# Arrays laid out in DRAM as on chip, with fewer loads, LoRA A summed on GpSimd and a planner that takes copy destinations in advance

## The chip, the cores and the metric

The kernel runs on one core of a Trainium2 chip. The metric is the device time of one execution in microseconds (us). The engines are called as in the profile: PE is TensorE (PEld its weight loads), DVE is VectorE, ACT is ScalarE, POOL is GpSimd, and SP is SyncE, which issues every load and store of this kernel.

## What is computed

The inputs are x (4 batches of 256 tokens with 512 features), a context of 64 rows per batch, four 256x256 side matrices per batch index (used as block weights) and a mask over the context rows. Four layers follow one another; the last two are the same function with the same arguments.

```python
# layer 0: routed LoRA; lora_A is the context, summed over its 4 batches
w   = softmax(x @ router_W.T + router_b)             # 8 experts
a   = einsum('bsh,arh->bsr', x, ctx)                 # x @ (sum of ctx over a).T
y   = einsum('bsr,nhr->bsnh', a, lora_B)
x   = nan_to_num(x + 0.5 * einsum('bsn,bsnh->bsh', w, y))
# layer 1: cross attention to ctx, 32 heads of 16, masked, then layer norm
x   = layernorm(x + attend(x @ Wq.T + bq, ctx @ Wk.T + bk, ctx @ Wv.T + bv, mask) @ Wo.T + bo) * ln_g + ln_b
# layers 2 and 3: 4 blocks each over the 8 nearest neighbours of the
# context's 512 columns; x is seen as 256 channels by 512 points
idx = top_k(-distance(ctx columns), 8)
for i in range(4):
    p = leaky_relu(x)
    x = (f[i] @ p + (f[i] @ gather(p, idx)).sum(8)) / 9 + x
```

## The kernel before

**Planner.** The kernel does not fix the order of its instructions by hand. Each step is added to a `Plan` with its engine, an estimated cost, what it reads and what it writes (`add`, L63). `emit` (L84) then plays the steps through: every engine has a time at which it is free, a step can start when its inputs are there and when its buffers have places, and among the steps of an engine that could start within 0.05 us of the earliest, the one with the lowest rank is issued. The rank is the due time of the batch, `DEADLINES = (0.0, 20.0, 40.0, 45.0)` (L32), minus the length of the work that still hangs on the step. A load's end is estimated from one pipe (L129). Buffers (`Buf`) come from pools with a fixed number of places: 8 PSUM banks, 5 halves (`half`, 128x512 f32), 4 `pT`, 8 `wp` and so on. A place is taken when the first step that names the buffer is issued. The result is one fixed queue of instructions per engine. On the chip each engine works through its queue in order and waits on semaphores where an operand is not ready.

**Loads.** SP issues all loads in the order in which the code lists them (L237 to L262). Most arrays are kept in the DRAM as plain matrices and are rearranged by the access pattern. xT, ctxT and the side matrices `fT` come in runs of 1 KB, weights and x in runs of 2 KB; the router's weights in runs of 32 bytes and the biases `bqk` in runs of 16 bytes.

**Work of one batch.** `mixture` multiplies xT by the router weights and the summed context (`route`, L327), takes a softmax over 8 experts on DVE and ACT (L341 to L352), forms `z` (L357), transposes it (`zT`, L375, copied by ACT, L380) and multiplies it by lora_BT (`upd`, L385). DVE adds the result to x (L400) and cleans it of NaNs with POOL's help (L406 to L410); a transpose gives `x1T` (L414, L420), and POOL adds bo (L426). `queries` makes the queries (`q`, L580), `values` the values (`v`, L542, put into `vbd` by DVE, L560), `keys` once the keys of all batches (`kT`, L488, spread by POOL into `kbd`, L511). `attention` scores (`s`, L610 and L621), takes the softmax (DVE L647, L653, L662, L668, L674; ACT L659; POOL L683), transposes (`pT`, L695, L700), and applies values (`avT`, L707, L721) and output weights (`o`, L727), followed by the layer norm (L739 to L752). `nearest` copies the context (`cxl`, POOL L431; its square, ACT L430), computes distances (`d`, L439), picks eight neighbours with DVE (`top` L445, `rest` L448, `near` L454) and turns the choice into a matrix `nbr` (L466 to L472). Each of 32 `block` steps computes the leaky ReLU on DVE (`p`, L765), a product with the side matrix (`wp`, L776), splits it into a high part (ACT, L789) and a low part (DVE, `wpl`, L792), gathers through `nbr` (`blk`, L807) and adds (DVE, L819).

The context summed over the batches (LoRA A) is one DVE reduction at L301, and the router's weights land straight beside it in the tile `rw`, so that one matmul gives logits and LoRA product:

```python
V_.tensor_reduce(rw[:, :, NB:], ctxT.rearrange("p c b v -> p c v b"), AX.X, ALU.add)
```

Of the kernel before, what the change touches and what calls it, by code (L numbers as in the profile page):

```python
# [18 lines left out]
V, R = 64, 64  # L19
# [12 lines left out]
DEADLINES = (0.0, 20.0, 40.0, 45.0)  # L32
# [5 lines left out]

class Buf:


    def __init__(self, kind, name):
        self.kind, self.name, self.users, self.left, self.tile = kind, name, [], 0, None
# [6 lines left out]
class Plan:  # L50
# [7 lines left out]
    def __init__(self, places, make):  # L58
        self.places = {k: [(0.0, i) for i in range(n)] for k, n in places.items()}
        self.make, self.ops, self.wrote, self.read = make, [], {}, {}  # L60
        self.batch, self.unit, self.pipe = 0, None, 0.0
# [22 lines left out]
    def emit(self, deadline):  # L84
# [16 lines left out]
        while ready:  # L101
            best = {}
            for op in ready:
                t = max([free[op.eng]] + [o.end + (SEEN[o.eng] if o.eng != op.eng else 0.0) for o in op.before])
                want = {}
                for k in op.bufs:
                    if k.tile is None:
                        want[k.kind] = want.get(k.kind, 0) + 1
# [6 lines left out]
            for eng, found in best.items():  # L115
                first = min(t for t, _ in found)
                t, op = min((f for f in found if f[0] <= first + 0.05), key=lambda f: (f[1].rank, f[1].n))
# [3 lines left out]
            for k in op.bufs:  # L121
                if k.tile is None:
                    self.places[k.kind].sort()
                    _, k.place = self.places[k.kind].pop(0)
                    k.tile = self.make(k.kind, k.place, k.name)
            op.fn()
            free[op.eng] = op.end = t + op.cost
            if op.load:
                self.pipe = op.end = max(op.end + 1.6, self.pipe) + op.load / 0.33  # L129
            for k in op.bufs:  # L130
                k.left -= 1
                if not k.left:
                    self.places[k.kind].append((op.end + (0.0 if op.load else SEEN[op.eng]), k.place))
# [8 lines left out]
def xattn_seq_kernel(ctx: ExitStack, tc: tile.TileContext, a: dict, out: bass.AP):  # L142
# [27 lines left out]
    plan = Plan({kind: n for kind, (_, _, _, n) in shapes.items()}, make)  # L170
# [29 lines left out]
    rbb = const.tile([128, NB], F32, name="rbb")  # L200
    bqk = const.tile([128, 2, NC], F32, name="bqk")
    mask_i = const.tile([128, B, V], I32, name="mask_i")
    rows = {n: const.tile([128, H], F32, name=n) for n in ("bv", "bo", "ln_g", "ln_b")}
# [19 lines left out]
    xT_src = a["xT"].rearrange("(c p) t -> p c t", p=128)  # L223
    x_src = a["x"].rearrange("(b l p) h -> b p l h", p=128, l=NL)

    def load_xT(b):

        after = (("x1T", 1, 0),) if b == B - 1 else ()
        load(xT[b], 0.5, lambda: xT[b].tile, xT_src[:, :, b * S : (b + 1) * S], after)

    def load_x(b):
        load(("x", b), 0.5, lambda: x1[b], x_src[b])

    def load_w(n):
        load(n, 1.0, lambda: w[n], a[n].rearrange("(c p) o -> p c o", p=128))

    load(("cxx", 0), 0.13, lambda: cxx[0][0:64], a["ctx"][0])  # L237
    load("ctxT", 0.5, lambda: ctxT, a["ctxT"].rearrange("(c p) (b v) -> p c b v", p=128, v=V))
    load("rw", 0.02, lambda: rw[:, :, 0:NB], a["router_WT"].rearrange("(c p) n -> p c n", p=128))
    load_xT(0)  # L240
    load("rbb", 0.01, lambda: rbb, a["router_b"].partition_broadcast(128))
    load_w("lora_BT")
    load_x(0)
    load("bqk", 0.02, lambda: bqk, a["bqk"].rearrange("k p c -> p k c"))
    for b in range(1, B):
        load(("cxx", b), 0.13, lambda b=b: cxx[b][0:64], a["ctx"][b])
    load("mask_i", 0.12, lambda: mask_i.rearrange("p b v -> p (b v)"), a["mask"].partition_broadcast(128))
    for c in range(NC):
        load(("WkT", c), 0.25, lambda c=c: WkT[c], a["WkT"][bass.ts(c, 128), :])
    load_w("WqT")  # L250
    load_w("WvT")
    load("bv", 0.25, lambda: rows["bv"], a["bv"].partition_broadcast(128))
    load_xT(1)
    load_x(1)
    load("bo", 0.25, lambda: rows["bo"], a["bo"].partition_broadcast(128))
    load_w("WoT")
    load("ln_g", 0.25, lambda: rows["ln_g"], a["ln_g"].partition_broadcast(128))
    load("ln_b", 0.25, lambda: rows["ln_b"], a["ln_b"].partition_broadcast(128))
# [630 lines left out]
```

## Time and profile before

| | us |
|---|---|
| median of 3 runs | 423.57 (423.35 to 423.77) |
| profiled execution, device time | 422.2 |
| its span, first to last instruction | 420.5 |
| PE busy | 400.4 (95%) |
| DVE busy | 287.6 (68%) |
| ACT busy | 115.0 (27%) |
| POOL busy | 93.8 (22%) |

The mean granted TensorE clock of the profiled execution is 0.992. The DMA queues move 15.19 MB in it, nearly all of the loads in the first 45 us. Busy time of an engine is the time that its instructions cover; matmuls are pipelined, and their ends are modelled. In the timeline each row has its start and its length in us, engine, line, operation, tiles and number of instructions; brackets hold the idle time of the engine just before, and what ended it. A float32 matmul appears as two instructions. In the chain of waits each row has a start, a length, and the engine and line that the end of the kernel hung on at that time.

### The profile page before, as it was taken

The page shows a single profiled execution, that of the slowest core. Times are in us where ns is not written, and L with a number is a line of the kernel's source. Part 1 is how long each engine was busy: PE and PEld are TensorE (multiplying, and loading weights), DVE is VectorE, ACT ScalarE, POOL GpSimd, SP SyncE. Part 2 cuts the span into 40 slices and gives each one's busy share as a digit, 9 for nine tenths or more (in the row PEclk, how much of TensorE's full clock was granted, in tenths as well). Part 3 has the DMA queues.
Part 4 walks back from the last instruction along what each step waited for, and adds up shares of the span by engine and source line. Part 5 has one row for each costly group of instructions (what it writes and reads, how often), then busy time and mean ns, then how long its engine had stood idle before and what let it go on. Part 6 is the DMA issues. An engine that isn't in the chain of part 4 may idle for free.

```text
span 420.5 us, 5667 instructions
## 1 busy us (share of the span) xinstructions
PE 400.4 (95%) x2288; PEld 305.8 (73%) x2288; DVE 287.6 (68%) x495; ACT 115.0 (27%) x210; POOL 93.8 (22%) x94
## 2 busy tenths in 40 slices
PE   5499998999999999988999999999999999999996
PEld 3358864678666588757758678788888888888885
DVE  4581699956999876999796676855546565555552
ACT  1203432611365023523445121131111112121211
POOL 4129031660306550263435022000000000000000
PEclk9799999999999999999999999999999999999999
DMA  6999200000000000000000000000100000000002
GB/s 201 251 343 354 67 0 2 2 1 0 2 1 2 2 0 2 0 2 0 2 2 2 0 0 0 2 0 2 50 1 2 0 2 0 25 27 0 0 2 100
DMA packets 10617, 15.19 MB, mean 36 GB/s; under 512 B 1504, under 2 KB 5216, under 8 KB 10592
## 3 DMA queue, kind: packets, MB, share of 16 engines
q1 hardware_dynamic: 10592, 14.84, 10.8%
q8 instruction: 18, 0.29, 0.3%
q14 instruction: 7, 0.06, 0.0%
HBM read 12.74 MB, written 2.10 MB: 35 GB/s over the span
## 4 chain that ended last, share of the span: by engine, by line
PE 81%; DVE 10%; DMA 2%; ACT 2%; SPq 2%; issue 1%; POOL 1%; ACTq 0%; DVEq 0%
PE blk L807 27%; PE wp L776 24%; PE o L727 7%; PE upd L385 6%; PE q L580 5%; PE pT L695 2%; DMA cxx<-in_ctx 2%; DVE p L765 2%; SPq L219 2%; PE d L439 2%; PE avT L707 1%; DVE den L662 1%; PE s L621 1%; DVE mx L647 1%; PE x1T L414 1%
## 5 line engine op out<-in xcount | busy, mean ns | idle before, releaser
L776 PE MATMUL wp<-fT,p 128*128 128x256 f32 x512 | 116.8, 380 | 1.5 <-DVE wpl L792 1.5
L807 PE MATMUL blk<-nbr,wph 128*128 128x512 f32 x256 | 107.8, 421 | 1.5 <-DVE wpl L792 1.5
L776 PEld LDWEIGHTS wp<-fT,p 128*128 128x128 f32 x512 | 96.2, 190 | 17.1 <-DVE wpl L792 1.9
L807 PE MATMUL blk<-nbr,wpl 128*128 128x512 f32 x256 | 100.5, 393 | 0.1
L789 ACT CAST wph<-wp 128x512 fp32r<-128x512 f32 x64 | 37.4, 585 | 161.5 <-PE wp L776 156.2
L792 DVE TENSOR_TENSOR wpl<-wp,wph 128x512 fp32r<-128x512 f32 x64 | 44.0, 690 | 49.7 <-ACT wph L789 49.4
L819 DVE SCALAR_TENSOR_TENSOR x<-blk,x 128x512 f32<-128x512 f32 x64 | 43.9, 687 | 36.3 <-PE blk L807 36.2
L807 PEld LDWEIGHTS blk<-nbr,wph 128*128 128x128 f32 x256 | 48.1, 188 | 13.8 <-DVE wpl L792 1.9
L807 PEld LDWEIGHTS blk<-nbr,wpl 128*128 128x128 f32 x256 | 48.2, 188 | 11.3 <-DVE wpl L792 0.6
L765 DVE SCALAR_TENSOR_TENSOR p<-x 128x512 f32<-128x512 f32 x64 | 50.4, 796 | 7.2 <-POOL x L752 5.8
L683 POOL TENSOR_TENSOR s<-s,rden 128x512 f32<-128x512 f32 x32 | 36.3, 1165 | 83.9 <-DVE rden L674 72.0
L385 PE MATMUL upd<-lora_BT,zTs 128*128 128x512 f32 x64 | 29.6, 606 | 0.9 <-ACT avTs L721 0.8
L647 DVE TENSOR_REDUCE mx<-s 128x8 f32<-128x512 f32 x32 | 19.8, 682 | 14.3 <-PE s L621 14.3
L727 PE MATMUL o<-WoT,avTs 128*128 128x512 f32 x64 | 29.0, 594 | 0.0
L580 PE MATMUL q<-x1T,WqT 128*128 128x256 f32 x128 | 28.5, 380 | 0.4 <-ACT x1T L420 0.4
L580 PEld LDWEIGHTS q<-x1T,WqT 128*128 128x128 f32 x128 | 24.2, 190 | 4.3 <-ACT x1T L420 0.6
L439 PE MATMUL d<-cxx,cxl 128*128 128x512 f32 x32 | 18.2, 698 | 7.3 <-POOL cxl L431 7.3
L700 ACT COPY pTs<-pT 128x512 f32<-128x512 f32 x32 | 17.1, 595 | 24.7 <-PE pT L695 24.1
L385 PEld LDWEIGHTS upd<-lora_BT,zTs 128*128 128x128 f32 x64 | 12.2, 197 | 13.7 <-issue 12.3
L727 PEld LDWEIGHTS o<-WoT,avTs 128*128 128x128 f32 x64 | 11.8, 190 | 12.3 <-issue 11.9
L662 DVE TENSOR_REDUCE den<-s 128x8 f32<-128x512 f32 x32 | 19.8, 678 | 0.3 <-ACT s L659 0.3
L653 DVE TENSOR_TENSOR s<-s,mx 128x512 f32<-128x512 f32 x32 | 20.0, 682 | 0.0
(86 smaller groups left out, 372.2 us busy)
## 6 DMA issues: line engine op xcount, KB each, us to landing
xT<-in_xT SPq DMA_DIRECT2D x4, 512.0 KB, 8.1
x<-in_x SPq DMA_DIRECT2D x4, 512.0 KB, 10.3
out<-x SPq DMA_DIRECT2D x8, 256.0 KB, 2.0
lora_BT<-in_lora_BT SPq DMA_DIRECT2D x1, 1024.0 KB, 11.0
WkT<-in_WkT SPq DMA_DIRECT2D x4, 256.0 KB, 4.9
WqT<-in_WqT SPq DMA_DIRECT2D x1, 1024.0 KB, 7.5
WvT<-in_WvT SPq DMA_DIRECT2D x1, 1024.0 KB, 9.5
WoT<-in_WoT SPq DMA_DIRECT2D x1, 1024.0 KB, 12.4
```

The source lines that it names most:

```text
L385: T_.matmul(ps2.tile, lhsT=zT.tile[:, bass.ts(c, 128)], rhs=w["lora_BT"][:, c, :], start=(c == 0), stop=(c == NC - 1),)
L439: lambda ps=ps, j=j: T_.matmul(ps.tile, lhsT=cxl[b][:, bass.ts(j, 128)], rhs=cxx[b], start=True, stop=True),
L580: T_.matmul(ps.tile[:, 0:S], lhsT=w["WqT"][:, c, bass.ts(o, 128)], rhs=x1T[b].tile[:, c, :], start=(c == 0), stop=(c == NC - 1),)
L647: lambda mx=mx, ps=ps: V_.tensor_reduce(mx.tile[:, 0:HPC], heads(ps), AX.X, ALU.max),
L683: lambda s=s, g=g: G_.tensor_tensor(heads(s), heads(s), rden.tile[:, bass.ts(g, HPC)].unsqueeze(2).to_broadcast([128, HPC, V]), ALU.mult,),
L727: T_.matmul(po.tile, lhsT=avT.tile[:, bass.ts(c, 128)], rhs=w["WoT"][:, c, :], start=(c == 0), stop=(c == NC - 1),)
L765: lambda l=l: V_.scalar_tensor_tensor(p.tile[:, l], pt[:, l], SLOPE, pt[:, l], ALU.mult, ALU.max),
L776: T_.matmul(ps.tile[:, bass.ts(k, S)], lhsT=p.tile[:, c, bass.ts(2 * m2 + k, 128)], rhs=wi[:, c, :], start=(c == 0), stop=(c == NL - 1),)
L789: act(0.59, lambda ps=ps, hi=hi: A_.copy(hi.tile, ps.tile), (ps,), (hi,))
L792: lambda ps=ps, hi=hi, lo=lo: V_.tensor_tensor(lo.tile, ps.tile, hi.tile.bitcast(F32), ALU.subtract),
L807: T_.matmul(pb[o].tile, lhsT=part.tile[:, bass.ds(m % 2 * S + o * 128, 128)], rhs=nbr[b, m], start=(m == 0 and k == 0), stop=(m == H // 12 ...
L819: lambda o=o: V_.scalar_tensor_tensor(pt[:, o], pb[o].tile, 1.0 / (KNN + 1.0), pt[:, o], ALU.mult, ALU.add),
```

## The change

The host lays the arrays out so that each partition's share is one run: 4 KB for xT, ctxT and x, 8 KB for lora_BT, the weights and the side matrices, with WkT still taken in four loads of 2 KB runs. Router weights, router_b and the q and k biases become one array `small` (192 bytes per partition), bv and bo one (`rows1`), ln_g and ln_b one (`rows2`). The context of batch 1 is loaded ahead of lora_BT, and the mask behind WqT. Since the router's weights no longer land in `rw`, ACT copies them there. The sum for LoRA A is made by three GpSimd additions of 128x256, with one `half` buffer for the two partial sums. In the planner, loads are modelled with eight in flight at a rate of 0.3 in place of 0.33, due times are changed, the 0.05 us tolerance is dropped, a second kind of place (`stage`, 8 of them) is counted beside the PSUM banks of all steps but the blocks, and several matmul steps name the SBUF buffer into which their PSUM result will be copied, so that its place is taken with the matmul. `values` names `vbd` in its matmul as well.

```diff
-DEADLINES = (0.0, 20.0, 40.0, 45.0)
+DEADLINES = (0.0, 5.0, 45.0, 50.0)
...
+LANES = 8
+RATE = 0.3
...
-                t = max([free[op.eng]] + [o.end + (SEEN[o.eng] if o.eng != op.eng else 0.0) for o in op.before])
+                t = free[op.eng] if not op.load else max(free[op.eng], self.landed[-LANES])
+                t = max([t] + [o.end + (SEEN[o.eng] if o.eng != op.eng else 0.0) for o in op.before])
...
-                t, op = min((f for f in found if f[0] <= first + 0.05), key=lambda f: (f[1].rank, f[1].n))
+                t, op = min((f for f in found if f[0] <= first), key=lambda f: (f[1].rank, f[1].n))
...
-                self.pipe = op.end = max(op.end + 1.6, self.pipe) + op.load / 0.33
+                op.end = max(op.end + 1.4, self.landed[-1]) + op.load / RATE
+                self.landed.append(op.end)
...
-    plan = Plan({kind: n for kind, (_, _, _, n) in shapes.items()}, make)
+    plan = Plan({kind: n for kind, (_, _, _, n) in shapes.items()} | {"stage": 8}, make)
...
-        load(xT[b], 0.5, lambda: xT[b].tile, xT_src[:, :, b * S : (b + 1) * S], after)
+        load(xT[b], 0.5, lambda: xT[b].tile.rearrange("p c t -> p (c t)"), a["xT"][b], after)
...
-        load(n, 1.0, lambda: w[n], a[n].rearrange("(c p) o -> p c o", p=128))
+        load(n, 1.0, lambda: w[n].rearrange("p c o -> p (c o)"), a[n])

     load(("cxx", 0), 0.13, lambda: cxx[0][0:64], a["ctx"][0])
-    load("ctxT", 0.5, lambda: ctxT, a["ctxT"].rearrange("(c p) (b v) -> p c b v", p=128, v=V))
-    load("rw", 0.02, lambda: rw[:, :, 0:NB], a["router_WT"].rearrange("(c p) n -> p c n", p=128))
+    load("ctxT", 0.5, lambda: ctxT.rearrange("p c b v -> p (c b v)"), a["ctxT"])
+    load("small", 0.05, lambda: consts, a["small"])
     load_xT(0)
-    load("rbb", 0.01, lambda: rbb, a["router_b"].partition_broadcast(128))
+    load(("cxx", 1), 0.13, lambda: cxx[1][0:64], a["ctx"][1])
     load_w("lora_BT")
     load_x(0)
-    load("bqk", 0.02, lambda: bqk, a["bqk"].rearrange("k p c -> p k c"))
-    for b in range(1, B):
+    for b in range(2, B):
         load(("cxx", b), 0.13, lambda b=b: cxx[b][0:64], a["ctx"][b])
+    for c in range(NC):
+        load(("WkT", c), 0.25, lambda c=c: WkT[c], a["WkT"][:, bass.ts(c, H)])
+    load_w("WqT")
     load("mask_i", 0.12, lambda: mask_i.rearrange("p b v -> p (b v)"), a["mask"].partition_broadcast(128))
-    for c in range(NC):
-        load(("WkT", c), 0.25, lambda c=c: WkT[c], a["WkT"][bass.ts(c, 128), :])
-    load_w("WqT")
     load_w("WvT")
-    load("bv", 0.25, lambda: rows["bv"], a["bv"].partition_broadcast(128))
+    load("rows1", 0.5, lambda: rows1, a["rows1"].partition_broadcast(128))
     load_xT(1)
     load_x(1)
-    load("bo", 0.25, lambda: rows["bo"], a["bo"].partition_broadcast(128))
     load_w("WoT")
-    load("ln_g", 0.25, lambda: rows["ln_g"], a["ln_g"].partition_broadcast(128))
-    load("ln_b", 0.25, lambda: rows["ln_b"], a["ln_b"].partition_broadcast(128))
-    load("fT", 1.0, lambda: fT, a["fsideT"].rearrange("i (c p) o -> p i c o", p=128))
+    load("rows2", 0.5, lambda: rows2, a["rows2"].partition_broadcast(128))
+    load("fT", 1.0, lambda: fT.rearrange("p i c o -> p (i c o)"), a["fsideT"])
...
     def lora_a():
-        dve(
-            1.9,
-            lambda: V_.tensor_reduce(rw[:, :, NB:], ctxT.rearrange("p c b v -> p c v b"), AX.X, ALU.add),
-            ("ctxT",),
+        act(
+            0.25,
+            lambda: A_.copy(rw[:, :, 0:NB], consts[:, 0 : NC * NB].rearrange("p (c n) -> p c n", n=NB)),
+            ("small",),
+            ("rw",),
+        )
+        part = Buf("half", "lora_a")
+
+        def half(k):
+            return part.tile[:, k * 256 : (k + 1) * 256].rearrange("p (c v) -> p c v", v=V)
+
+        for k in range(2):
+            pool(
+                0.66,
+                lambda k=k: G_.tensor_tensor(half(k), ctxT[:, :, 2 * k, :], ctxT[:, :, 2 * k + 1, :], ALU.add),
+                ("ctxT", part),
+                (("part", k),),
+            )
+        pool(
+            0.66,
+            lambda: G_.tensor_tensor(rw[:, :, NB:], half(0), half(1), ALU.add),
+            (part, ("part", 0), ("part", 1)),
             ("rw_a",),
         )
...
             (("z", b, l), zb, "ident"),
-            (ps,),
+            (ps, zT),
...
             ("WvT", "ctxT"),
-            (ps,),
+            (ps, ("vbd", b % 2)),
```

The copy's buffer is named in the same way in the matmul steps of `pT` (L695), `avT` (L707) and `wp` (L776, with both the high and the low part).

## The prediction

> **What bounds the kernel now.** I read the page first, then a table of engine time by stage, then the waits, the timeline and the chain of waits of the first 60 us. The page's first part names the bound.
>
> ```profile
> span 420.5 us, 5667 instructions
> PE 400.4 (95%) x2288; PEld 305.8 (73%) x2288; DVE 287.6 (68%) x495; ACT 115.0 (27%) x210; POOL 93.8 (22%) x94
> ```
>
> PE is busy for 400.4 of 420.5 us, so 20.1 us of idle PE, and whatever PE does slowly, is all that can be won without removing matmuls; the change removes none. The stage table, cut where the trace changes character, says where those 20.1 us lie (busy us per engine, then granted clock, DMA share, GB/s).
>
> ```profile
> 0.00:20.43 20.43, 10.56 (x34) 6.08 (x35) 9.41 (x23) 4.51 (x7) 6.81 (x22) 0.86 0.79 224
> 20.43:45.65 25.22, 24.59 (x134) 18.24 (x133) 11.08 (x23) 5.43 (x11) 12.97 (x12) 0.98 0.88 304
> 45.65:90.00 44.35, 42.03 (x321) 27.52 (x322) 41.99 (x83) 17.95 (x35) 16.52 (x14) 1.00 0.05 13
> 90.00:250.00 160.00, 156.45 (x1039) 115.45 (x1038) 129.35 (x220) 57.07 (x106) 52.25 (x43) 1.00 0.00 1
> 250.00:416.40 166.40, 166.40 (x766) 138.55 (x764) 94.96 (x148) 30.07 (x53) 5.25 (x4) 1.00 0.03 10
> 416.40:420.50 4.10, 0.36 (x2) 0.00 (x0) 0.84 (x2) 0.00 (x0) 0.00 (x0) 1.00 0.33 128
> ```
>
> Stage length minus PE busy: 9.87, 0.63, 2.32, 3.55, 0 and 3.74 us. Half is in the first 20 us. The timeline and the chain of waits show why.
>
> ```profile
> 4.30 5.48 PE L439 MATMUL d<-cxx,cxl 128*128 128x512 f32 x8 [4.30 <-POOL cxl L431]
> 9.62 1.90 PE L327 MATMUL route<-rw,xT 128*128 128x72 f32 x16
> 14.07 0.66 PE L375 MATMUL zT<-ident,z 128*128 128x128 f32 x4 [2.56 <-DVE z L357]
> 17.74 2.05 PE L439 MATMUL d<-cxx,cxl 128*128 128x512 f32 x2 [3.01 <-POOL cxl L431]
> 20.43 7.62 PE L385 MATMUL upd<-lora_BT,zTs 128*128 128x512 f32 x16
> 4.87 2.77 SPq L219 DMA_DIRECT2D bqk<-in_bqk  x1
> 7.68 9.31 DMA cxx<-in_ctx
> 17.05 0.61 POOL cxl L431
> ```
>
> PE starts at 4.30, as soon as the first context is copied. It idles 2.56 us for z, which comes from a chain of small DVE operations, and then 3.01 us because the next instruction in its queue is a distance matmul of batch 1, whose context was issued behind lora_BT, x and bqk and lands only at 16.99. `upd` stands behind it. lora_BT is no excuse: issued at 3.65 with 11.0 us to landing, it is there at 14.65.
>
> **Change, part by part.** *Order of the loads.* The context of batch 1 moves ahead of lora_BT, into the place where router_b was issued at 3.11. xT of batch 0, just ahead of it, lands at 7.96 (2.56 + 5.4). With 128 KB more I put cxx1 at 8.5 to 9.5; router_b itself, in that place, landed at 10.7 (3.11 + 7.6), which is my late end. POOL's copy (0.60) and ACT's square (0.63) follow, so the distances of batch 1 can start between 9.1 and 11.3, before route ends at 11.52 (9.62 + 1.90). They are 8 matmul instructions of 0.43 us, 3.4 us in all, and fill PE while DVE makes z. z is ready at 14.0 as now: its chain from route is unchanged, and DVE's interleaved match is worth at most 0.7 us either way. Then zT (0.43), ACT's copy (0.59) and handovers: `upd` starts at 15.2 to 15.8, and I take 15.5 instead of 20.43: 4.9 us. With lora_BT at 14.65, or later by the 0.4 us that 128 KB cost at 300 GB/s, this still holds. By then three quarters of the batch-1 distance matmuls, which now run at 53.64 (six instructions, 2.6 us), are also behind us; the 4.9 us count the displacement of `upd`, and this is extra work pulled forward, worth up to 2.6 us if the stage at 45 to 90 us stays full.
>
> *Clock.* The granted clock fell in the gaps:
>
> ```profile
> 12.00:16.00 4.00, 0.66 (x4) 0.42 (x4) 2.52 (x8) 0.22 (x1) 0.00 (x0) 0.85 0.95 192
> 16.00:20.00 4.00, 2.26 (x4) 1.15 (x5) 1.41 (x4) 2.39 (x4) 1.76 (x3) 0.50 0.80 255
> 20.00:24.00 4.00, 4.00 (x11) 2.06 (x10) 3.99 (x12) 0.59 (x1) 0.00 (x0) 0.80 1.01 336
> ```
>
> Sixteen `upd` matmuls took 7.62 us where the steady 0.43 us give 6.9: 0.7 us to win. The two slow distance matmuls (2.05 for 0.86) lie inside the interval already counted. [...] The row shows 0.50 directly behind the two gaps with 0.66 us of work between, so I take the row: front gain 5.6.
>
> *LoRA A on GpSimd.* Removed: one DVE reduction, 1.93 us from 5.74. Added: three POOL adds of 128x256. The nearest row is POOL's 128x512 add at 1327 ns (L408), half of it 0.66 each, 2.0 in sum; the strided 128x256 product at 1005 ns (L511) gives 3.0 as the high end. ctxT lands at 5.7, so the sum is ready at 7.7 to 8.7, later than now or equal, but before route's 9.62, held by PE's own distances. [...] If POOL's three remaining memsets go first (they end at 6.42 now), 8.4 to 9.4, still in time. ACT gains one copy of 128x32, near the 0.22 us of its small exponent, before route, on an engine that is idle from 4.2 to 12.2 now: nothing. DVE's MAX8 can start 1.9 us sooner; nobody on PE waits for them before 45 us.
>
> *Longer runs, fewer loads.* SP loses four issues (router weights, router_b and bqk become one load, bv joins bo, ln_g joins ln_b); bqk alone held SP 2.77 us. The queue moved 192 GB/s at 12 to 16 us and 336 afterwards. If long runs change nothing, the loads land as now; if they bring 300 to 350 GB/s from 5 us on, lora_BT lands near 11 and WkT near 17. In neither case does PE meet a load: through WkT 4.2 MB are queued, against 5.4 MB that had landed by 24.5 us (WqT, 17.0 + 7.5). WkT comes by about 21 now (last issue 16.4, median 4.9 to landing), and kT would start at 22.4 (15.5 + 6.9). A loss is excluded only by that 1.4 us. The mask moves behind WqT. DVE waits for it today for 3.88 us; if its wait falls in front of x (L400), due at 19 instead of 26.37, up to 2 us are lost on DVE, covered by kT's 6.9 us on PE. I charge nothing.
>
> *Planner.* Later due time for batches 2 and 3 (40, 45 to 45, 50), earlier for batch 1 (20 to 5), no 0.05 tolerance, PSUM copies' destinations reserved with the matmul, v reserved until vbd is free. These only reorder the same instructions. The stage of 45 to 90 is bound by DVE (41.99 of 44.35) while DVE idles 14 us in the stage before. Batch 1's z (1.3 us the pair) and the matches of its distances (about 7 us) can now move into that hole. I book 1.3 of the 2.32 idle us there, and nothing for 90 to 250, where the idle 3.55 may shrink to nothing or double. v for batch 2, which held a bank from 60.12, no longer does.
>
> **Sum.** 4.9 + 0.7 + 1.3 = 6.9 us. Span 413.6; the profiled execution takes 1.7 more around its span (422.2), so 415.3. The median of the runs shown is 1.4 above that execution (423.57): 416.7.
>
> **Rivals.**
> 1. *Given back in the DVE-bound stage* (20 in 100). PE reaches the softmax 5.6 us sooner, but the distances that filled PE at 53.64 have been spent, so PE waits for rden and POOL's product. For it: DVE busy 95% there. Against it: DVE work goes forward too. It returns 2.6 plus the 1.3: gain 3.0, 420.6.
> 2. *Slower through DVE's queue* (14 in 100). With batch 1 due at 5, its softmax runs level with batch 0's blocks, and each block's low-part subtraction (L792) stands behind reductions. The trace has one such place, 185 to 195 us, where PE waited 1.48 and 1.46 us:
>
> ```profile
> 188.89 1.99 PE L776 MATMUL wp<-fT,p 128*128 128x256 f32 x8 [1.48 <-DVE wpl L792]
> 192.34 0.50 PE L807 MATMUL blk<-nbr,wph 128*128 128x512 f32 x1 [1.46 <-DVE wpl L792]
> ```
>
> At 2.94 us a block it decides from three further blocks (6.9 / 2.94 = 2.3); four give 11.8 - 6.9 = 4.9 lost, 428.5. Against it: 90 to 250 has DVE at 81%.
> 3. *The front does not move* (5 in 100): cxx1 lands late after all, or the planner puts another late operand in front of `upd`; 423.6.
> 4. The forecast case (61 in 100), alone 412 to 420; its low end also empties the idle of 90 to 250.
>
> **Numbers.** A difference below 0.2% (0.85 us) is about what cannot be told from no change here. Faster: cases 4 and 1, 0.80 after a little spill. Same: 0.05. Slower: 0.15. The range runs from 411.0 (the front's 5.6, all of the 2.3 and 3.5 us of later idle, and 1 of the 2 us by which the first eight distances, 5.48 us, exceed their steady 3.4) to 423.5, leaving out most of rival 2.
>
> **What would show it.** Right: batch-1 distances between 11.5 and 15 us; `upd` from 15 to 16; no granted clock near 0.50 at 16 to 20; POOL adds done before route; PE idle before 20 us about 5. Wrong: an `upd` start after 18, a wait on WkT, mask or small in front of kT or x, or more than 6 us of PE idle between 45 and 250, above all on wpl.

## The result, and the profile after

| | us (median, lowest to highest) |
|---|---|
| before | 423.46 (422.39 to 423.77, 4 runs) |
| after | 428.85 (427.95 to 429.03, 4 runs) |
| ratio after / before | 1.0128 (95% interval 1.0105 to 1.015) |

The change makes the kernel 1.3% slower, where 416.7 us had been forecast. The profiled execution of the changed kernel took 428.73 us at a mean granted clock of 0.982; before it had been 422.2 us at 0.992. First the head of the page of the kernel after.

```profile
span 427.0 us, 5667 instructions
PE 404.3 (95%) x2288; PEld 307.3 (72%) x2288; DVE 281.0 (66%) x494; ACT 116.1 (27%) x211; POOL 94.8 (22%) x97
```

PE runs the same 2288 matmul instructions in 404.3 us instead of 400.4, and it is idle for 22.7 us instead of 20.1. So both its idle time and its own pace got worse. The stage table of after, cut at the same places as that of before (busy us and instructions of PE, PEld, DVE, ACT and POOL, then granted clock, DMA share, GB/s), says where.

```profile
0.00:20.43 20.43, 16.39 (x50) 8.58 (x51) 12.96 (x32) 5.34 (x9) 9.17 (x25) 1.00 0.91 300
20.43:45.65 25.22, 24.57 (x119) 18.38 (x121) 14.26 (x35) 5.65 (x12) 13.31 (x12) 1.00 0.67 263
45.65:90.00 44.35, 36.93 (x307) 25.78 (x303) 35.31 (x68) 16.91 (x32) 14.09 (x12) 0.92 0.00 1
90.00:250.00 160.00, 153.17 (x983) 112.79 (x976) 119.59 (x211) 51.20 (x92) 40.57 (x35) 0.98 0.00 1
250.00:416.40 166.40, 166.40 (x821) 136.37 (x820) 95.74 (x148) 35.79 (x64) 17.70 (x14) 1.00 0.02 7
416.40:427.00 10.60, 6.86 (x31) 5.43 (x29) 3.18 (x5) 1.17 (x2) 0.00 (x0) 0.94 0.26 99
```

Stage length minus PE busy gives the idle time: 4.04, 0.65, 7.42, 6.83, 0 and 3.74 us, where before it was 9.87, 0.63, 2.32, 3.55, 0 and 3.74. The front won 5.8 us, as forecast. The two stages behind the loads lost 5.1 and 3.3 us, and PE's own time grew by 3.9 us: -5.8 + 5.1 + 3.3 + 3.9 = 6.5, the whole difference of the spans. Nearly all of the loss lies between 45 and 120 us. That stretch of the kernel before, and then of the kernel after, in the same columns:

```profile
45.00:120.00 75.00, 72.68 (x538) 50.67 (x531) 63.85 (x123) 26.10 (x49) 23.13 (x20) 1.00 0.03 8
```

```profile
45.00:120.00 75.00, 61.18 (x478) 39.72 (x478) 59.94 (x117) 29.06 (x53) 26.23 (x24) 0.92 0.00 1
```

PE is idle for 2.32 us of it before and for 13.82 us after, and over the whole stretch DVE is less busy too. That mean hides two parts. Cut where DVE stops, the kernel after shows them:

```profile
45.41:81.36 35.95, 28.53 (x253) 19.37 (x250) 35.55 (x68) 14.40 (x27) 14.09 (x12) 0.91 0.00 1
81.36:90.66 9.30, 9.30 (x73) 7.18 (x71) 0.00 (x1) 2.51 (x6) 0.00 (x0) 1.00 0.01 2
```

First DVE works almost without a gap (35.55 of 35.95 us), and PE waits for it; then PE works without a gap, and DVE has nothing to do. The waits of PE in the kernel after (total us, times, longest) name three that lie in this stretch: the first, third and fourth rows (the second is the start of the kernel).

```profile
PE v L572 <- issue: 4.7, 1, 4.7
PE d L469 <- POOL cxl L461: 4.0, 1, 4.0
PE o L757 <- DVE s L683: 3.3, 1, 3.3
PE upd L415 <- ACT zTs L410: 3.1, 2, 2.5
```

The timeline of after shows how the first arises and what PE and DVE do around the third.

```profile
45.53 1.06 PE L651 MATMUL s<-kbd,qT 32*128 32x128 f32 x32
46.64 1.06 PE L651 MATMUL s<-kbd,qT 32*128 32x128 f32 x32
46.88 4.87 DVE L677 TENSOR_REDUCE mx<-s 128x8 f32<-128x512 f32 x8
51.67 4.86 DVE L683 TENSOR_TENSOR s<-s,mx 128x512 f32<-128x512 f32 x8
52.45 5.90 PE L572 MATMUL v<-WvT,ctxT 128*64 128x256 f32 x32 [4.75 <-issue]
...
80.18 7.07 PE L610 MATMUL q<-x1T,WqT 128*128 128x256 f32 x32
90.66 2.48 DVE L677 TENSOR_REDUCE mx<-s 128x8 f32<-128x512 f32 x4 [9.30 <-PE s L651]
100.99 5.37 PE L757 MATMUL o<-WoT,avTs 128*128 128x512 f32 x8 [3.25 <-DVE s L683]
```

Both halves of batch 0 are scored within 2.2 us. Each half takes four PSUM banks, so all eight are full. DVE then takes eight maxima before the first of eight subtractions, and only a subtraction gives a bank back. The values' matmul `v` needs one and starts at 52.45, just after the first subtraction (51.67 plus about 0.6). The trace writes "issue", since it found no event that released it. Behind the softmax of both halves DVE makes batch 1's `z` and x (the steps of `mixture`); PE needs them for `x1T` and the queries `q`, which start at 80.18. Only behind `q` do the next scores come, so DVE stands idle for 9.30 us until 90.66, and then PE stands idle for 3.25 us until DVE has subtracted. Behind the idle the granted clock is low (0.61, 0.68 and 0.68 over the three groups that follow): 32 matmuls of `v` take 5.90 us, eight of `o` 5.37 us, and eight of `upd` at 117.90 5.40 us, where the same groups take 3.67, 3.70 and 3.70 us in a kernel without these gaps (the seven-place kernel below). These three cost 2.2 + 1.7 + 1.7 = 5.6 us, more than the 3.9 us by which PE's whole time grew; the front's better clock (1.00 in the first 20.43 us, where it had been 0.86) gave a part back.

### The profile page after: what moved, and what is told of

It is laid out like the page before. It is cut to its first block, busy times and chain, and to the rows that moved or that the text cites. A ratio compares the mean times of both kernels' runs of the same rounds, so it can differ in the third digit from the quotient of the medians.

```text
span 427.0 us, 5667 instructions
## 1 busy us (share of the span) xinstructions
PE 404.3 (95%) x2288; PEld 307.3 (72%) x2288; DVE 281.0 (66%) x494; ACT 116.1 (27%) x211; POOL 94.8 (22%) x97
## 4 chain that ended last, share of the span: by engine, by line
PE 91%; DVE 4%; ACT 2%; issue 2%; POOL 1%; DMA 1%; POOLq 0%; ACTq 0%
PE blk L837 28%; PE wp L806 26%; PE o L757 7%; PE q L610 6%; PE upd L415 6%; PE d L469 4%; PE pT L725 3%; PE v L572 2%; PE avT L737 2%; PE s L651 2%; PE route L357 1%; PE nbrT L496 1%; PE kT L518 1%; PE x1T L444 1%; PE zT L405 1%
## 5 line engine op out<-in xcount | busy, mean ns | idle before, releaser
L795 DVE SCALAR_TENSOR_TENSOR p<-x 128x512 f32<-128x512 f32 x64 | 47.9, 751 | 3.0 <-POOL x L782 1.4
L757 PE MATMUL o<-WoT,avTs 128*128 128x512 f32 x64 | 31.1, 626 | 3.3 <-DVE s L683 3.3
L415 PE MATMUL upd<-lora_BT,zTs 128*128 128x512 f32 x64 | 30.8, 626 | 3.1 <-ACT zTs L410 3.1
L456 POOL TENSOR_TENSOR x<-x,rows 128x512 f32<-128x512 f32 x8 | 10.2, 1280 | 62.4 <-PE x1T L444 62.4
L757 PEld LDWEIGHTS o<-WoT,avTs 128*128 128x128 f32 x64 | 12.2, 199 | 15.6 <-issue 15.2
L689 ACT ACTIVATE s<-s 128x512 f32<-128x512 f32 x32 | 18.7, 630 | 16.7 <-DVE s L683 16.7
L730 ACT COPY pTs<-pT 128x512 f32<-128x512 f32 x32 | 17.3, 596 | 14.7 <-PE pT L725 14.6
```

The costliest lines, as they stand in the source:

```text
L415: T_.matmul(ps2.tile, lhsT=zT.tile[:, bass.ts(c, 128)], rhs=w["lora_BT"][:, c, :], start=(c == 0), stop=(c == NC - 1),)
L757: T_.matmul(po.tile, lhsT=avT.tile[:, bass.ts(c, 128)], rhs=w["WoT"][:, c, :], start=(c == 0), stop=(c == NC - 1),)
L795: lambda l=l: V_.scalar_tensor_tensor(p.tile[:, l], pt[:, l], SLOPE, pt[:, l], ALU.mult, ALU.max),
```

## The experiments

Two theories stood at first. **Banks**: batch 0's two halves take all eight PSUM banks and PE waits for one. **Due times**: batch 1 due at 5 brings its work level with batch 0's, and the two ask DVE at once. The rival to both was that longer runs or the other loads had done the harm.

**Seven places instead of eight.** The steps of all but the blocks share `stage` places. With eight, the count of them never binds before the eight banks do. With seven, the second half can't be scored while the first holds four.

```diff
-    plan = Plan({kind: n for kind, (_, _, _, n) in shapes.items()} | {"stage": 8}, make)
+    plan = Plan({kind: n for kind, (_, _, _, n) in shapes.items()} | {"stage": 7}, make)
```

> The kernel after with one number changed: 7 places of the kind stage in place of 8, so that the planner can't issue the scores of two token halves (four PSUM banks each) side by side. Theory banks: in the kernel after, two such pairs take all eight banks, at 45 to 52 us and at 96 to 101 us, and PE stands 4.75 and 3.25 us until DVE's first subtraction frees a bank; with the slow clock behind them (v 5.90 for 3.9 us, o 5.37 for 3.4 us) they cost about 12 us, so this kernel takes 415 to 419 us, with no PE wait above 2 us between 40 and 110 us. Theory due times (batch 1 due at 5 makes DVE's queue serve two softmaxes while the blocks starve): the due times are still there, so 426 to 430 us. Theory front (GpSimd sum, long runs or more ACT work cost time): nothing of it is changed, 426 to 430 us.

Measured: 414.37 us against 422.72, ratio 0.9798 (0.9776 to 0.982), so 14.5 us below the kernel after; measured again, 414.33 (0.9801, 0.9776 to 0.9826). The timeline of this kernel at the place of the wait and at batch 1's queries, and its two stages:

```profile
46.41 3.67 PE L572 MATMUL v<-WvT,ctxT 128*64 128x256 f32 x32
46.78 2.48 DVE L677 TENSOR_REDUCE mx<-s 128x8 f32<-128x512 f32 x4
49.17 2.47 DVE L683 TENSOR_TENSOR s<-s,mx 128x512 f32<-128x512 f32 x4
...
72.17 7.17 PE L610 MATMUL q<-x1T,WqT 128*128 128x256 f32 x32
72.93 2.47 DVE L677 TENSOR_REDUCE mx<-s 128x8 f32<-128x512 f32 x4
```

```profile
45.65:90.00 44.35, 41.85 (x364) 29.27 (x360) 43.25 (x84) 20.19 (x39) 13.66 (x12) 1.00 0.01 1
90.00:250.00 160.00, 157.23 (x1044) 118.02 (x1037) 126.90 (x215) 56.77 (x103) 53.32 (x43) 1.00 0.00 1
```

DVE takes four maxima and then four subtractions, `v` does not wait, and the clock stays at 1.00. Batch 0's second half is scored only at 71.18, so DVE comes to batch 1 sooner: `q` starts at 72.17, not 80.18, and DVE has that second half to work on meanwhile. Idle PE time is 2.50 and 2.77 us in the two stages, against 7.42 and 6.83 in the kernel after. Of the 14.7 us between the two spans, 8.8 are idle PE time and 5.9 slower matmuls (404.3 us of PE against 398.4). All loads and the GpSimd sum are those of the change, so they are not what made it slow. Several edits of the planner can move the order; the next runs tell them apart.

**The second half made to wait.** The same effect as seven places, at one place only: batch 0's second half is scored after the first half's subtractions.

```diff
-            (*(("qT", b, o) for o in range(NC)), qT, "mbias", "ones", *(("kbd", o, k) for o in range(NC) for k in range(2))),
+            (*((("sub", b, 0, g) for g in range(NG)) if l and b in (0,) else ()), *(("qT", b, o) for o in range(NC)), qT, "mbias", "ones", *(("kbd", o, k) for o in range(NC) for k in range(2))),
...
-                (s,),
+                (s, ("sub", b, l, g)),
```

> The kernel after with one added dependence: the scores of the second token half of batch 0 are issued after DVE's subtractions of the first half. It takes away the first of the two full-bank places only (45 to 52 us); the rest of the plan can shift. Theory banks: at least the first wait (4.75 us) and the slow v behind it (2.0 us) go, so 422 us or less. Theory due times: an added dependence can only delay DVE's work, 428 to 431 us. Theory front: 428 to 430 us.

Measured: 414.66 against 422.72, ratio 0.9803 (0.9786 to 0.9821). It looks like proof of the bank theory. It is not: with the new dependence the planner also ordered everything behind it anew.

**The due times of before.**

```diff
-DEADLINES = (0.0, 5.0, 45.0, 50.0)
+DEADLINES = (0.0, 20.0, 40.0, 45.0)
```

> The kernel after with the due times of before (0, 20, 40, 45). The queue of PE still has the two score groups of batch 0 side by side, those of batch 1 are apart. Theory banks: the first full-bank wait of about 5 us stays at 42 to 50 us, the second (3.25 us and the slow o behind it, 5.2 in all) goes: 421 to 424 us. Theory due times: nearly everything comes back, and the front's gain of about 6 us shows: 415 to 418 us. Theory front: 426 to 430 us.

Measured: 413.70 against 422.72, ratio 0.9781 (0.9758 to 0.9804): better than either theory had put it. The waits of this kernel, and its stages behind the loads:

```profile
PE zT L405 <- DVE s L683: 4.7, 1, 4.7
```

```profile
45.65:90.00 44.35, 40.12 (x252) 27.81 (x253) 35.09 (x71) 18.76 (x37) 19.08 (x16) 0.96 0.00 1
90.00:250.00 160.00, 159.95 (x1082) 119.58 (x1081) 128.41 (x218) 57.78 (x106) 53.12 (x44) 1.00 0.00 1
```

The pair of batch 0 is still there, and PE still waits 4.7 us for a subtraction behind eight maxima; only the waiting instruction is another (`zT`). Yet the kernel is as fast as with seven places, since from 90 to 250 us PE hardly stands still (0.05 us). So the bank theory as stated falls: one such wait of 4.7 us is not what makes 428.9 out of 414.

**The front alone.** The kernel after with the planner of before: its tolerance, due times, rate and no reservation of copies' places, so that loads, layouts and the GpSimd sum are left.

```diff
-DEADLINES = (0.0, 5.0, 45.0, 50.0)
+DEADLINES = (0.0, 20.0, 40.0, 45.0)
...
-                t = free[op.eng] if not op.load else max(free[op.eng], self.landed[-LANES])
+                t = free[op.eng]
...
-                t, op = min((f for f in found if f[0] <= first), key=lambda f: (f[1].rank, f[1].n))
+                t, op = min((f for f in found if f[0] <= first + 0.05), key=lambda f: (f[1].rank, f[1].n))
...
-                op.end = max(op.end + 1.4, self.landed[-1]) + op.load / RATE
+                op.end = max(op.end + 1.6, self.landed[-1]) + op.load / 0.33
...
-            (ps, zT),
+            (ps,),
```

(`pT`, `avT`, `wp` and `v` in the same way.)

> The kernel after with the planner of before (due times, tolerance 0.05, rate 0.33 from one pipe, no copy places taken in advance, vbd not named in the values' matmul): only the layout, the loads and their order, and LoRA A on GpSimd are left of the change. In its queue the score groups of batches 0 and 1 are apart and those of batch 2 stand side by side. Theory banks: front gain of 5 to 6 us, one full-bank wait of about 5 us near 160 us: 420 to 424 us. Theory due times: no loss left, 416 to 418 us. Theory front: the loss is in these parts, 427 to 430 us.

Measured: 419.42 against 422.72, ratio 0.9916 (0.9892 to 0.994). Loads, layouts and the GpSimd sum bring 3.3 us under the planner of before, so the planner's edits together cost about 9 us (428.85 against 419.42, in separate measurements). The time lies just outside what each of the three theories had asked. Its front is that of the kernel after (PE busy 16.35 of the first 20.43 us), so some 2.5 of the front's 5.8 us are given back: at 162 us this order has a pair of halves of its own, and PE waits 4.9 us for it.

```profile
PE wp L806 <- DVE s L683: 4.9, 1, 4.9
```

**The order of one load alone, in the kernel before.**

```diff
+    load(("cxx", 1), 0.13, lambda: cxx[1][0:64], a["ctx"][1])
     load_w("lora_BT")
...
-    for b in range(1, B):
+    for b in range(2, B):
```

> The kernel before with one load moved: the context of batch 1 ahead of lora_BT, in the place that it has in after; layout, loads, LoRA A on DVE and the planner stay as before. Its queue order behind the front is nearly that of the run with only the layout, loads and LoRA A of after (419.4 us). If the order of that one load makes the front's gain, PE starts upd at 15 to 18 us and the time is 418.5 to 420.5 us. If the long runs or the GpSimd sum made it, upd stays near 20 us and the time is 423 us or above.

Measured: 422.40 (420.39 to 425.74, 20 runs) against 422.78, ratio 1.0003 (0.9983 to 1.0022): no change, and the expectation missed. PE's idle time in the first 20.43 us fell from 9.87 to 6.9 us, not to 4, for a new wait (first row): ACT's copy of `zT` stands behind its squares. The 3 us that remain are spent again at the same pair, here at 166 us (second row), and the time comes out even.

```profile
PE zT L376 <- ACT zTs L381: 2.3, 1, 2.3
PE wp L777 <- DVE s L654: 4.9, 1, 4.9
```

**The new due times alone, in the kernel before.**

```diff
-DEADLINES = (0.0, 20.0, 40.0, 45.0)
+DEADLINES = (0.0, 5.0, 45.0, 50.0)
```

> The kernel before with the due times of after (0, 5, 45, 50) and nothing else. Its PE queue then has the two score groups of batch 0 side by side and batch 1 close behind. Theory due times: they alone cost what the kernel after lost against its front gain, 5.4 + 5.8 = 11 us: 431 to 436 us. Theory lockstep as an interplay of due times with the missing bank limit: one full-bank wait of 5 us, partly filled, 424 to 429 us. Theory banks: 427 to 429 us.

Measured: 427.51 against 422.78, ratio 1.0115 (1.0083 to 1.0147). The due times do harm without any of the rest, 4.7 us, though not the 11 that their theory had asked, and the largest new wait is again for a subtraction:

```profile
PE q L580 <- DVE s L653: 4.5, 1, 4.5
```

**The bank wait taken out of a frozen order.** To settle whether the wait at 52.45 costs what it shows, the order of the kernel after was written down and played back, with one thing moved. In the first kernel batch 0's second-half scores and softmax stand behind the first half's subtractions; in the second DVE subtracts directly behind each maximum in batches 0 and 1.

```diff
+ORDER = [
+    0, 24, 1, 30, 31, 2, 33, 32, 35, 3, 34, 4, 26, 5, 195, 196, 6, 25, 197, 7, 36, 8, 27, 201,
...
+            want_n = ORDER[done]
+            done += 1
+            t, op = next(f for found in best.values() for f in found if f[1].n == want_n)
```

> The kernel after with every engine's order written out as its planner made it, and only this moved: in batch 0 the scores of the second token half, and its softmax on DVE and ACT, stand behind the whole softmax of the first half. No other instruction changes its place. Theory banks (the full-bank wait of 4.75 us at 45 to 52 us is itself the cost): that wait and the slow v behind it go, 421 to 424 us. Theory lockstep (batch 0's halves and batch 1 ask for DVE at the same time and leave PE without independent work; the bank wait is only where it shows first): PE waits as long further on, for DVE's later steps, 427 to 430 us.

> The kernel after with every engine's order written out, PE's, ACT's and POOL's unchanged, and on DVE in batches 0 and 1 each score group's subtraction directly behind its maximum, so that the first of the eight banks comes free after 1.2 us of DVE instead of 4.9 us. Theory banks: PE's wait of 4.75 us shrinks by 3.6 us, the later one of 3.25 us by 1.8 us, and their slow matmuls go with them: 421 to 425 us. Theory lockstep: the waits move to a later step of DVE, 427 to 430 us.

Measured: 427.64 and 428.43 against 422.78, ratios 1.0137 (1.0104 to 1.0169) and 1.0155 (1.0122 to 1.0188). The long wait of `v` is gone from both, and the time is that of the kernel after. PE in the first, then in the second:

```profile
58.93 8.42 PE L520 MATMUL d<-cxx,cxl 128*128 128x512 f32 x12 [3.16 <-DVE s L734]
80.92 7.07 PE L661 MATMUL q<-x1T,WqT 128*128 128x256 f32 x32
```

```profile
55.96 3.29 PE L408 MATMUL route<-rw,xT 128*128 128x72 f32 x16 [0.92 <-PE nbrT L549]
59.04 7.42 PE L520 MATMUL d<-cxx,cxl 128*128 128x512 f32 x12
80.83 7.07 PE L661 MATMUL q<-x1T,WqT 128*128 128x256 f32 x32
```

In the first, 3.16 us come back on the next instruction in PE's queue that needs the same DVE work, and the low clock with them (0.7 in the slice of 53.5 to 64.2 us of its page): the twelve distances take 8.42 us, where the kernel after has 5.36. In the second the waits are short and many (0.69 to 0.92 us), and `route` and the distances are slow all the same (3.29 for 1.96, 7.42 for 5.36, with 0.6 in the slice of 53.3 to 63.9 us). Both kernels come to batch 1's `q` when the kernel after does, at 80.9 and 80.8 us: the same softmax work of DVE stands in front of it in either order. So removing the wait that the profile names largest won nothing.

**One microsecond more.** The due times once more: batch 1 due at 6 instead of 5.

```diff
-DEADLINES = (0.0, 5.0, 45.0, 50.0)
+DEADLINES = (0.0, 6.0, 45.0, 50.0)
```

> The kernel after with batch 1's due time at 6 in place of 5, nothing else. If the slow plan is a coincidence of one setting, a neighbour lands elsewhere, at 414 to 422 us. If it belongs to this kind of planner setting (8 places and batch 1 due close to batch 0): 426 us or slower.

Measured: 441.64 against 422.93, ratio 1.0448 (1.0408 to 1.0489): slower still, with three waits of 4.5 to 4.8 us instead of one.

```profile
PE v L572 <- issue: 4.8, 1, 4.8
PE pT L725 <- DVE s L683: 4.5, 1, 4.5
PE wp L806 <- DVE s L683: 4.5, 1, 4.5
```

So 428.9 is no single unlucky order. With batch 1 due about as early as batch 0 and eight places, the orders that come out are poor; the later due times or one place fewer, each alone, repair it.

**Values that don't name `vbd`.**

```diff
-            (ps, ("vbd", b % 2)),
+            (ps,),
```

> The kernel after, 8 stage places and its due times, where only the values' matmul no longer names vbd in the planner, so that the values of batches 2 and 3 can be made early again. Theory that due times and 8 places alone make the two token halves and the two batches run in step: 426 to 430 us. Theory that PE's lack of independent work between 45 and 120 us is the loss, and that any edit which hands it some gives most of it back: 418 to 424 us, with the values of batch 2 before 100 us.

Measured: 421.09 against 422.93, ratio 0.9956 (0.9941 to 0.9971). All 64 `v` instructions run between 52.5 and 65 us, and 7.8 of the 14 us come back, though PE's 4.8 us wait for a bank stays. In the kernel after, the `v` of batch 2 runs at 106.29, behind the 3.25 us gap, and that of batch 3 at 224.71; so the reservation takes independent work away from the stretch where PE starves. That this is how it costs the 7.8 us is inferred, since the order behind it changes too; the seven-place kernel keeps the reservation, has the `v` of batch 2 at 95.54, and loses nothing.

**The softmax's maximum left out.** If PE waits for DVE's softmax in the kernel after and not in the seven-place kernel, less DVE work must help the one and not the other. In both kernels the maximum over the context rows is left out of the computation, and the subtraction becomes a clamp that reads the same bank.

```diff
-                lambda mx=mx, ps=ps: V_.tensor_reduce(mx.tile[:, 0:HPC], heads(ps), AX.X, ALU.max),
+                lambda: None,
...
-                lambda mx=mx, ps=ps, s=s: V_.tensor_tensor(
-                    heads(s), heads(ps), mx.tile[:, 0:HPC].unsqueeze(2).to_broadcast([128, HPC, V]), ALU.subtract
-                ),
+                lambda ps=ps, s=s: V_.tensor_scalar(s.tile, ps.tile, 80.0, -80.0, ALU.min, ALU.max),
```

> The kernel after in its own order on every engine, with the 32 maxima of the softmax (DVE, 128x512, about 0.62 us each back to back) left out and the subtraction replaced by a clamp of the scores: part of the computation is left out. Theory in step (between 45 and 120 us PE waits for DVE's softmax because both halves and both batches ask for it at once): 16 maxima, 9.9 us of DVE, lie in front of PE's waits in that stretch, so PE busy there rises from 61 us to 68 or more and the time falls by 7 to 12 us, to 417 to 422 us. Theory order (PE's own queue or ACT and POOL chains make the idle time, DVE is a bystander): the time falls by less than 3 us, 426 us or more.

> The same left out of the kernel with 7 stage places. There PE idles only 4.3 us between 45 and 120 us. Theory in step: DVE is no longer what PE waits for, so the same 20 us less of DVE work bring at most 2 to 4 us: 410.5 to 412.5 us. Theory that DVE's load as such is the bound of that stretch in either order: as large a gain as in its neighbour, 7 us or more, 407 us or less.

Measured: 419.84 from after, ratio to before 0.9936 (0.9916 to 0.9957), and 413.56 from the seven-place kernel, 0.9786 (0.9771 to 0.9801): 9.0 us less the one, 0.8 us the other. DVE lost 18.8 us (281.0 to 262.2) and 17.8 us (286.2 to 268.4) of busy time. First the stretch of 45 to 120 us of the kernel after with the maximum left out, then that of the seven-place kernel, complete (its second measurement):

```profile
45.00:120.00 75.00, 66.17 (x542) 43.06 (x541) 59.16 (x118) 32.03 (x59) 30.15 (x26) 0.98 0.01 1
```

```profile
45.00:120.00 75.00, 70.66 (x568) 45.32 (x567) 71.48 (x133) 33.25 (x61) 30.57 (x26) 1.00 0.01 1
```

The time fell as much as the theory of waits for the softmax had asked (7 to 12 us), PE's busy time less (to 66.17 us, not 68). Batch 1's `q` started at 75.65 instead of 80.18, so the eight maxima that had stood in front of it (4.87 us) did set its start; in the seven-place kernel it moved by 0.8 us, from 72.17 to 71.40. This shows the mechanism: the kernel after is bound in this stretch by how long PE waits for DVE's softmax, although DVE is only 80% busy over the whole of it (59.94 of 75), and the seven-place kernel is not, although its DVE is 95% busy (71.48 of 75). What differs is when the softmax is asked for and what else PE has in its queue meanwhile. It has to be read from the waits and from the cut at 81.36 us; the busy shares of the whole stretch point to the wrong kernel. 6.3 us between the two kernels remain without the maxima.

**Shorter runs.** The seven-place kernel with every array kept as a plain matrix again, so that the loads come in runs of 1 to 2 KB; each engine's queue is otherwise the same, instruction for instruction.

```diff
-        load(n, 1.0, lambda: w[n].rearrange("p c o -> p (c o)"), a[n])
+        load(n, 1.0, lambda: w[n], a[n].rearrange("(c p) o -> p c o", p=128))
```

(xT, x, ctxT, WkT and the side matrices in the same way.)

> The fastest kind of version so far once more, with more rounds and on the chip that runs the next kernel: the kernel after with 7 stage places. From 414.4 us before: 413.5 to 415.5 us, ratio 0.977 to 0.983.

> The same with 7 stage places and the same loads in the same order, but the arrays in the DRAM as plain matrices again, read in runs of 1 or 2 KB per partition; every engine's queue is the same as in its neighbour. If the length of the runs lies off the critical path (lora_BT lands before z is ready in either layout): within 0.5 us of its neighbour. If the long runs are part of the front's gain (the front with the load of batch 1's context moved alone had upd at 18.8 us, with the whole layout at 17.2): 1 to 3 us slower, with later upd.

Measured side by side: 414.33 (0.9801, 0.9776 to 0.9826) and 415.29 (0.9826, 0.98 to 0.9851). The packets, of the kernel with long runs, then with short ones:

```profile
DMA packets 4665, 15.19 MB, mean 37 GB/s; under 512 B 672, under 2 KB 800, under 8 KB 4000
```

```profile
DMA packets 9529, 15.19 MB, mean 37 GB/s; under 512 B 672, under 2 KB 4384, under 8 KB 9504
```

Twice the packets cost about 1 us: the intervals of the two ratios overlap, but all six measurements with short runs (414.77 to 416.25) lie above all six with long ones (414.06 to 414.73). That falls between the two expectations, and `upd` did not come later (17.13 against 17.48 us). No larger gain from longer runs was measured.

**What beats both kernels.** Seven places, or the old due times, with all the rest of the change: 414.3 and 413.7 us, 2% below before.

## Why the prediction was wrong

**The front: right.** The context of batch 1 had landed by 8.96 us (forecast 8.5 to 9.5), its distances run at 11.85, the clock does not fall (1.00 in both stages up to 45.65 us), and PE's idle time in the first 20.43 us is 4.04 us ("about 5"). Timeline of after:

```profile
11.85 3.65 PE L469 MATMUL d<-cxx,cxl 128*128 128x512 f32 x8
15.06 1.19 ACT L460 ACTIVATE cxx<-cxx 64x512 f32<-64x512 f32 x2 [1.99 <-DMA cxx<-in_ctx]
15.34 0.60 PE L405 MATMUL zT<-ident,z 128*128 128x128 f32 x4
16.28 0.59 ACT L410 COPY zTs<-zT 128x512 f32<-128x512 f32 x1
17.16 7.03 PE L415 MATMUL upd<-lora_BT,zTs 128*128 128x512 f32 x16
```

The start of `upd` was mis-sized: 17.16, not 15.5. Most of that lay in the forecast's own sum: eight distances of 3.4 us behind a `route` that ends at 11.52 fill PE until 14.9, but `zT` was put at 14.0, when z is ready. It ran at 15.34, behind the distances (`route` had started 0.5 us later, too). The last 0.3 us or so are ACT's: its squares of the contexts of batches 2 and 3 (15.06, 1.19 us) stand in front of its copy of `zT`. PE put two more distances (15.79) into that gap, so the idle time came out as forecast all the same. How much of the front reaches the end depends on the order behind it: 3.3 us with the planner of before.

**The clock: right.** Sixteen `upd` took 7.03 us instead of 7.62: 0.6 of the 0.7 us. The prediction took the low clock for the gaps' doing from one row of before, 0.50 directly behind two of them. The kernel after has a clearer case: a gap of 4.75 us, and the row of the five microseconds in which it ends reads 0.52.

```profile
50.00:55.00 5.00, 2.55 (x12) 1.65 (x14) 5.00 (x9) 2.62 (x5) 0.00 (x0) 0.52 0.00 0
117.90:123.30 5.40, 5.40 (x12) 2.10 (x16) 5.33 (x11) 0.00 (x0) 3.70 (x4) 0.68 0.00 0
```

The second row follows a single gap of 2.47 us and reads 0.68 over 5.4 us.

**LoRA A: right.** Each addition took 0.70 to 0.72 us (0.66 forecast), the last ended at 7.51, and `route` started at 10.12, held by PE's distances.

**Loads: right.** PE waits for no load after the first, nor for mask, `small` or WkT.

**The planner: the step that failed.** It reads: "These only reorder the same instructions … I book 1.3 of the 2.32 idle us there, and nothing for 90 to 250, where the idle 3.55 may shrink to nothing or double." The argument was one of busy time: DVE bounds 45 to 90, so DVE work that moves into the hole before it gives time back. The DVE work did move: DVE's busy time in the first 45.65 us rose from 20.5 to 27.2 us, and that of 45.65 to 90 fell from 41.99 to 35.31. PE's idle time there rose from 2.32 to 7.42 us all the same, and from 3.55 to 6.83 in the next stage. The new order puts the softmax of batch 0's second half on DVE ahead of the steps that batch 1's `q` needs, so DVE is full up to 81.36 us while PE waits, and empty for the 9.30 us after it. Sums of busy time do not see that: PE stops where its next instruction needs DVE work that is not yet done, here for 4.75 us before 52.45 and for 3.25 us before 100.99, and nothing else is in front of it. "Reorder" was the whole risk, and it was priced at a gain of 1.3 us. The runs put a loss of about 9 us there for all the planner's edits together (428.85 against 419.42 with the front alone), and 14.5 against the same kernel with one place fewer; the due times alone, in the kernel before, cost 4.7. The prediction's own sign of being wrong, more than 6 us of PE idle between 45 and 250, came: it was 14.3.

**Rival 2** had the sign, the trigger (batch 1 due at 5) and, at 428.5, nearly the number, but not the mechanism. It expected blocks' low parts (`wpl`) to stand behind reductions; the kernel after has no long wait on `wpl`, and its first `wp` starts at 131.0 us. Its waits are on the softmax's subtractions and on what hangs on them. The number is a coincidence. **Rival 1** (gain given back in the DVE-bound stage) named the engine that PE would wait for, and DVE is indeed full up to 81.36 us; but it still counted on a gain of 3.0 us, and did not see the 9.30 us without DVE work that follow. **Rival 3** did not happen.

**What stays open.** The later `q` alone is not enough to make a kernel slow: with the old due times it starts at 81.01 us, but there PE has batch 0's blocks from 87.9 on, which the kernel after starts at 131.0. Nor are late blocks enough: in the seven-place kernel they start at 117.3 and cost nothing. How the 14.5 us divide between the two, the waits behind 90 us and the clock was not separated by a run. Nor is the 1 us of shorter runs located in the trace. How much of the 14.5 us each planner edit holds is not a sum either: due times (15.2), places (14.5) and `vbd` (7.8) each undo much of the same loss.

## What to carry to other kernels

Where a planner turns costs and due times into fixed queues, a change of a due time or of a count of places is not a small edit: here one microsecond of batch 1's due time moved the kernel from 428.9 to 441.6 us, and one place fewer moved it to 414.4. Try such settings on the chip, each apart from the change that they come with, since otherwise a good change of the loads (-9 us with the old due times) is thrown away with a bad order. And if removing the largest wait of a profile leaves the time as it was, look at both engines' busy time in the stretch: if both have fallen, cut it where one of them stops, since they may be full in turn, here DVE up to 81 us and PE after it. Then what counts is the sum of work queued in front of the next hand-over, and not the wait that shows first.

## What was not expected of the hardware

- Behind one PE gap of 4.75 us the granted clock was low (0.52 in the row of 50 to 55 us), and 32 matmuls took 5.90 instead of 3.67 us: the gap cost half as much again as it lasted. A gap of 2.47 us had 1.7 us behind it. Behind the 4.66 us gap of the kernel with the old due times four `zT` took 1.08 us, where four at 69.43 us took 0.65; the clock was 0.96 from 45.65 to 90 us.
- The clock was low behind short gaps too: in the kernel with DVE's maxima and subtractions in pairs no wait of PE between 47 and 56 us is longer than 0.92 us, and the granted clock was 0.6 in the page's slice of 53.3 to 63.9 us, with PE busy without a gap from 55.96 to 66.46.
- The same kernel, the one with the one load moved, ran in 420.39 us at a mean granted clock of 0.996 and in 425.74 at 0.98. Its queues are fixed, so the order of instructions does not make this spread of 1.3%, and it goes with the clock: the five fastest of its 20 runs have 0.992 to 0.996, the five slowest 0.980 to 0.984.
- The loads reached 415 GB/s in one of the page's 40 slices of the kernel after; the best slice before had 354.
